# Grouping the score products of an attention pair, and dealing PSUM banks one by one

## The chip, the cores and the metric

The kernel runs on one core of a Trainium2 chip. A core has a matrix engine (TensorE, "PE" in the profile; its weight loads are "PEld"), a vector engine (VectorE, "DVE"), an engine for activations (ScalarE, "ACT"), a general one (GpSimd, "POOL"), a queue engine (SyncE, "SP") that here only issues DMAs, and 16 DMA engines. Matrix products are written to PSUM, an accumulator memory of 8 banks; a bank holds 512 float32 numbers on each of 128 partitions. The metric is the device time of one execution in microseconds (us), the median of several runs.

## What is computed

Eight sequences of 512 tokens of width 256 go through an attention layer with 16 heads of 64 and then through a gated feed-forward network with two hidden layers of 1024. All is float32. Only the attention part bears on the change:

```python
q = (x @ w_q).reshape(b, s, h, -1).transpose(0, 2, 1, 3)
kv = x @ w_kv
k, v = jnp.split(kv, 2, axis=-1)
...
q = _l2norm(q) * jnp.exp(scale)
k = _l2norm(k)
sim = jnp.einsum('bhid,bhjd->bhij', q, k)
attn = jax.nn.softmax(sim, axis=-1)
out = jnp.einsum('bhij,bhjd->bhid', attn, v)
out = out.transpose(0, 2, 1, 3).reshape(b, s, h * out.shape[-1])
return out @ w_out + b_out
...
x = x + _layernorm(_L0_attn_ref(_layernorm(x, axis=-1), ...), axis=-1)
x = x + _layernorm(_L0_ffn_ref(_layernorm(x, axis=-1), ...), axis=-1)
```

## The kernel before

**Stages.** The attention stage takes all eight sequences ("batches", `b`) one after the other, then the feed-forward network takes them in pairs. The attention stage writes its result to DRAM, and the feed-forward stage reads it back.

**Pairs.** Attention runs over 64 units of two heads, called pairs here, `(b, p)` with `p` from 0 to 7. Pairs 0 to 3 take the heads of the first half (`hf` 0), pairs 4 to 7 those of the second. For a pair:

- `scores(b, p, jb)` (lines 734 to 766), for each of four blocks `jb` of 128 keys: one product for each of the two heads (line 743), each with 64 rows of the array, so that both heads' products share it. The result `s` is a tile of two banks from the pool `ps_s`, which has two such tiles. Then ACT makes two exponentials (line 758), one for each head, into `e`; the key's inverse norm `kn` is the scale. There are five buffers of `e`, four of which a pair fills.
- `summed` (line 775), on DVE: the four blocks of `e` are added up in three additions into `es`.
- `values(b, p, jb)` (line 795): for each block and head a product with 64 columns of the array, accumulated over the four blocks in `po`, which has one bank (`ps_o`). `values_out` (line 891) copies it to `oT` on ACT. There are ten buffers of `oT`, eight of which a batch fills.
- `row_sums` (line 819), once for two pairs: the sums over keys, in products with 32 columns of the array, into `pd`; a copy `d`, a DMA that folds it, a reciprocal, a DMA to DRAM and two back spread it as `rden`, with which `normalised` (line 901) multiplies `oT`. Pairs 6 and 7 of the last batch use products with 64 columns and a reciprocal in place (`inverted`).

**Work beside the pairs.** Everything else of the stage is cut into steps, dealt to the pairs by the table `BESIDE` (lines 981 to 990), one string for each pair of a batch:

- `x`: a quarter of the next batch's input norm, with two transposes (`pt_a`, line 364).
- `t`: sums of tokens that the chains need.
- `c`: one product of a chain. A chain (`qk_chain`, from line 519; products at line 541) computes the queries or the keys of four pairs from seven products of quarter matrices in place of eight. Its products accumulate in PSUM banks called `g1`, `g2`, `g3`, and between them ACT copies a bank (`kept`, line 566), DVE adds a bank to a part made earlier (`added`, line 576), and ACT squares the result (`squared`, line 584). A product that goes on accumulating in a bank has to wait until the copy or addition of what is there has been done. There are four chains for each batch from the second on; the first is projected at the start.
- `q` and `k`: the sums of squares of queries or keys, in products with 32 columns (`norms_step`, line 633). For queries four DMAs, DVE work and a power on POOL (line 315) follow, and four DVE multiplications scale `qT`.
- `m`: the key norms: four transposes (`pk`, line 704), a DVE step and a power on POOL give `kn`.
- `v`: a quarter of the values of four pairs (`vp`, line 408), and a copy on ACT.
- `o`: a quarter of the output projection of the batch before (`pa`, line 922): eight products, then a norm on DVE and POOL.
- `l`: the issue of a load of a later batch.

Sums of the feed-forward weights (lines 1084 to 1140) also run there, on DVE and DMA; PE has no part in them.

**Order.** All steps are recorded by `steps.add(engine, length, run, reads, writes, takes, tiling)`. `Steps.issue` (line 84) then issues them. PE takes its steps strictly in the order in which they were recorded. Each other engine takes, of the steps that a model of the timing has ready, the one with the earliest latest start; what a step waits for follows from the parts of tiles that it reads and writes, and from the buffers that it takes.

For pair `u` and the pair ahead `n` the recorded order, which is PE's order, is: scores of `n`, blocks 0 and 1; values of `u` in four blocks; row sums at every second pair; scores of `n`, blocks 2 and 3; then the steps beside. The loop is at lines 1205 to 1234.

**PSUM.** Of the eight banks `ps_o` has one, `ps_s` four (two tiles of two), and `ps_w` three (`w0` to `w2`), which all other products share. `wbank` (line 325) deals these out, the least recently used first; a chain holds two of them (`hold=True`) from its first product to its last.

```python
    wbanks, held = [0, 1, 2], set()

    def wbank(hold=False):
        k = next(k for k in wbanks if k not in held)
        wbanks.remove(k)
        wbanks.append(k)
```

Below stand the functions that the diff touches, with the line numbers of the profile.

Of the kernel before, what the change touches and what calls it, by code (L numbers as in the profile page):

```python
# [17 lines left out]
P = 128  # L18
# [121 lines left out]
def tile_fast(  # L140
# [179 lines left out]

    wbanks, held = [0, 1, 2], set()

    def wbank(hold=False):
        k = next(k for k in wbanks if k not in held)
# [192 lines left out]
    def qk_chain(b, hf, which):  # L519
# [4 lines left out]
        g, tags = [("g1", *n), ("g2", *n), ("g3", *n)], {}  # L524

        def product(k, a, x, bank, fresh, last=False):
            if bank not in tags:
                tags[bank] = wbank(hold=True)
            tag = tags[bank]
            key = g[2] if k == 2 else g[bank]  # L530

            def run():
                if fresh:
                    tile_of(ps_w, [P, 2, HS], tag, key)
                w = quarter(which, hf, a)
                if x[0] == "T":
                    rhs = T[t][:, int(x[1]) - 1, :]
                else:
                    rhs = T["aT", b][:, int(x[1]) - 1, ts(int(x[2]) - 1, HS)]
                for o in range(2):  # L540
                    nc.tensor.matmul(  # L541
                        T[key][:, o, :], lhsT=w[:, ts(o, P)], rhs=rhs,
                        start=(fresh and o == 0), stop=True, skip_group_check=True,
                    )
# [12 lines left out]
            return key  # L557

        def part(i, k):
# [174 lines left out]
    def scores(b, p, jb):  # L734

        hf, j = divmod(p, HP)
        qT, kT, s, e = ("qT", b, hf), ("kT", b, hf), ("s", b, p, jb), ("e", b, p, jb)

        def products():
            tile_of(ps_s, [P, 2, S], "s", s)  # L740
            for h in range(2):
                hp = slice(h * DH, (h + 1) * DH)
                nc.tensor.matmul(  # L743
                    T[s][:, h, :],
                    lhsT=T[kT][hp, j, ts(jb, P)],
                    rhs=T[qT][hp, j, :],
                    start=True,
                    stop=True,
                )
# [5 lines left out]
        def exponentials():  # L755
            tile_of(ep, [P, 2, S], "e", e)
            for h in range(2):
                nc.scalar.activation(  # L758
                    T[e][:, h, :], T[s][:, h, :], AF.Exp,
                    scale=T["kn", b, hf][:, jb, 2 * j + h : 2 * j + h + 1],  # L760
                )

        steps.add(
            "act", 1.2, exponentials,
            reads=[(s, 0), (("kn", b, hf), 0)], writes=[(e, 0)], takes=[("e", NE, e)],
        )

    def summed(b, p, jb):

        t = ("es", b, p)  # L770

        def run():
            if jb == 1:
                tile_of(esp, [P, 2, S], "es", t)
            nc.vector.tensor_tensor(  # L775
                T[t], T["e", b, p, 0] if jb == 1 else T[t], T["e", b, p, jb], ALU.add
            )

        blocks = (0, 1) if jb == 1 else (jb,)
        steps.add(  # L780
            "dve", 1.22, run, reads=[(("e", b, p, i), 0) for i in blocks],
            writes=[(t, 0)], takes=[("es", 2, t)] if jb == 1 else (),
        )

    def values(b, p, jb):

        hf, j = divmod(p, HP)
        v, e, po = ("v", b, hf), ("e", b, p, jb), ("po", b, p)

        def products():  # L790
            if jb == 0:
                tile_of(ps_o, [P, S], "o", po)
            for h in range(2):
                c0 = j * P + h * DH
                nc.tensor.matmul(  # L795
                    T[po][h * DH : (h + 1) * DH, :],
                    lhsT=T[v][:, jb, c0 : c0 + DH],
                    rhs=T[e][:, h, :],
                    start=(jb == 0),
                    stop=(jb == NT - 1),  # L800
                )

        steps.add(
            "pe", 0.86, products, reads=[(e, 0), (v, jb)], writes=[(po, 0)],
            takes=[("o", 1, po)] if jb == 0 else (), tiling=("col", DH),
        )

# [97 lines left out]
    def out_proj(b, t, pairs=(0, NP), tail=False):  # L905

        pm, a, x = ("pa", b, t // 2 if tail else t), ("a", b, t), ("xres", b)
        st, mv, rs = ((n, b, t) for n in ("ost", "omv", "ors"))  # L910
        bank = None if tail else wbank()

        def banks():
            return T[pm][:, t % 2, :D] if tail else T[pm]

        def products():
            if pairs[0] == 0 and not tail:
                tile_of(ps_w, [P, D], bank, pm)
            elif pairs[0] == 0 and t % 2 == 0:
                tile_of(ps_s, [P, 2, S], "s", pm)  # L920
            for p in range(*pairs):
                nc.tensor.matmul(  # L922
                    banks(),
                    lhsT=T["oT", b, p][:, ts(t, P)],
                    rhs=wo_sb[:, p, :],
                    start=(p == 0),
                    stop=(p == NP - 1),
                )

        def biased():  # L930
            tile_of(rows, [P, D], "a", a)
            nc.vector.tensor_tensor(T[a], banks(), bo_sb, ALU.add)  # L932

        def stats():
            tile_of(small, [P, 6], "st1", st)
# [11 lines left out]

        takes = ()
        if pairs[0] == 0:
            takes = [(bank, 1, pm)] if not tail else [("s", 2, pm)] if t % 2 == 0 else ()  # L950
# [40 lines left out]
    plan = {}  # L991

# [206 lines left out]
        if t == 2:  # L1199
            key_norms(0, 1)  # L1200
    units = [(b, p) for b in range(B) for p in range(NP)]
    for g in range(2):
        for jb in (2 * g, 2 * g + 1):
            scores(*units[0], jb)
    for k, u in enumerate(units):
        ahead = units[k + 1 : k + 2]
        for jb in range(1, NT):
            summed(*u, jb)
        for g in range(2):
            for n in ahead:  # L1210
                for jb in (2 * g, 2 * g + 1):
                    scores(*n, jb)
            if g == 0:
                for jb in range(NT):
                    values(*u, jb)
                if not ahead:
                    for t in range(2):
                        out_proj(B - 1, t, (0, NP - 1), tail=True)
                b, p = u
                if (b, p // 2) == (B - 1, HP - 1):  # L1220
                    inverted(b, p)
                elif p % 2:
                    inverted_two(b, p - 1)
# [12 lines left out]
    for t in range(NT):  # L1236
# [3 lines left out]
    steps.add("pe", 0.0, lambda: None, reads=halves, tiling="full")  # L1240
    steps.add(
        "act", 1.5, lambda: nc.scalar.activation(top, top, AF.Silu),
        reads=[(("e", *units[-1], NT - 1), 0)],
    )
    for t in range(NT):
        out_proj(B - 1, t, (NP - 1, NP), tail=True)
    with tc.manual_schedule(engines=ORDERED):

        pm = ps_w.tile([P, S], F32, tag="w0", name="idle")
# [1000 lines left out]
```

## Time and profile before

| | us |
|---|---|
| median of 3 runs | 1607.86 (1606.53 to 1608.01) |
| the profiled execution | 1609.5 |
| its span, from the first to the last instruction | 1607.7 |
| PE busy in the span | 1587.7 |
| DVE, ACT, POOL busy | 1054.8, 927.8, 489.5 |
| values' last products in the attention stage | 985.9 |
| first product of the feed-forward stage | 1002.4 |

How to read it. The profile is of one execution. A row of a timeline has the start, the length, the engine, the line, what is written from what, the part of the array that is used (rows by columns), the shape and how many instructions were merged. A float32 product shows as two `MATMUL` instructions, since it is made in two passes. Starts are what was recorded; the ends of products are modelled, as products are pipelined, so a row may end after the next has begun. "Idle before" and the engine behind `<-` tell how long the engine had nothing to do and what ended it.

The PE clock that was granted is 0.996 of full speed in the mean of the span.

The groups that touch the change: 512 exponentials (line 758) have 316.7 us of ACT in all, 1024 score passes (line 743) 255.9 us of PE, 1024 value passes (line 795) 233.8 us, and the 192 sums of exponentials (line 775) 156.3 and 78.3 us of DVE.

### The profile page before, as it was taken

Reading aid. Unit: us, or ns where it says so; the run is one execution under the profiler, and the core shown is the slowest. Engines: PE = TensorE matmul, PEld = TensorE weight load, DVE = VectorE, ACT = ScalarE, POOL = GpSimd, SP = SyncE. Lnnn points to the kernel's source line nnn. Section 1 sums busy time; section 2 is a strip of 40 time slices with the busy share of each in tenths; the row PEclk is TensorE's granted clock in tenths of the full one; section 3 lists DMA queues with packets and bytes.
Section 4 is the critical chain, followed back from the end, with each engine's and each line's share of the span. In section 5 each row is a group of like instructions: output and inputs, shape, how many; then the busy total and the mean of one; then the engine's idle time right before and its main releaser. Section 6 shows DMA issues by size and latency. Waiting matters only on the chain.

```text
span 1607.7 us, 19708 instructions
## 1 busy us (share of the span) xinstructions
PE 1587.7 (99%) x7208; PEld 984.4 (61%) x7208; DVE 1054.8 (66%) x1772; ACT 927.8 (58%) x1543; POOL 489.5 (30%) x354
## 2 busy tenths in 40 slices
PE   9999999999999999999999999999999999999997
PEld 4344554454554554554554445788888888888886
DVE  4576776677454554554544365869787887879686
ACT  4666556556656556656646644566467646655663
POOL 4211312312302212212112120546165325625451
PEclk9999999999999999999999999999999999999998
DMA  5224323433211211121111310454324523441440
GB/s 175 54 80 124 110 97 94 119 106 80 54 40 41 48 46 41 42 53 41 41 53 41 93 54 19 143 155 147 120 77 131 170 92 103 145 139 60 140 149 29
DMA packets 77829, 142.66 MB, mean 89 GB/s; under 512 B 18844, under 2 KB 34460, under 8 KB 73628
## 3 DMA queue, kind: packets, MB, share of 16 engines
q1 hardware_dynamic: 58140, 78.40, 17.5%
q0 software_dynamic: 18880, 61.87, 12.4%
q8 instruction: 58, 0.95, 0.3%
q10 hardware_dynamic: 704, 1.05, 0.2%
q14 instruction: 47, 0.39, 0.1%
HBM read 123.49 MB, written 17.29 MB: 88 GB/s over the span
## 4 chain that ended last, share of the span: by engine, by line
PE 91%; DVE 4%; DMA 3%; ACT 1%; issue 1%; SPq 0%; DVEq 0%; ACTq 0%
PE g L1503 25%; PE s L743 14%; PE po L795 13%; PE p L1429 7%; PE vp L408 6%; PE pa L922 6%; PE g_k L541 5%; PE g_q L541 5%; PE py L1617 4%; PE pd L819 2%; DMA rden<-r 1%; DVE es L775 1%; PE pn_k L633 1%; PE pn_q L633 1%; PE kp L434 1%; PE qp L434 1%
## 5 line engine op out<-in xcount | busy, mean ns | idle before, releaser
L758 ACT ACTIVATE e<-s,kn 128x512 f32<-128x512 f32 x512 | 316.7, 686 | 183.4 <-PE s L743 144.6
L743 PE MATMUL s<-qT,kT 64*128 64x512 f32 x1024 | 255.9, 616 | 2.6 <-ACT e L758 2.4
L1503 PE MATMUL g<-h,wb_S 128*128 128x512 f32 x1024 | 234.2, 389 | 0.0
L795 PE MATMUL po<-e,v 128*64 128x512 f32 x1024 | 233.8, 598 | 0.0
L1503 PEld LDWEIGHTS g<-h,wb_S 128*128 128x128 f32 x1024 | 192.0, 188 | 39.8
L315 POOL TENSOR_TENSOR nf_q<-nf_q,neghalf 128x32 f32<-128x32 f32 x16 | 88.0, 5502 | 379.6 <-DVE nf_q L667 379.6
L775 DVE TENSOR_TENSOR es<-es,e 128x1024 f32<-128x1024 f32 x128 | 156.3, 1221 | 63.1 <-ACT e L758 57.6
L743 PEld LDWEIGHTS s<-qT,kT 64*128 64x128 f32 x1024 | 87.6, 186 | 145.4 <-issue 106.0
L1503 PE MATMUL g<-h,wb_A 128*128 128x512 f32 x768 | 176.4, 390 | 0.0
L775 DVE TENSOR_TENSOR es<-e,e 128x1024 f32<-128x1024 f32 x64 | 78.3, 1224 | 140.3 <-PE pd L819 102.4
L795 PEld LDWEIGHTS po<-e,v 128*64 128x64 f32 x1024 | 67.8, 136 | 158.2 <-issue 151.1
L1503 PEld LDWEIGHTS g<-h,wb_A 128*128 128x128 f32 x768 | 143.9, 188 | 29.9
L315 POOL TENSOR_TENSOR kn<-kn,neghalf 128x32 f32<-128x32 f32 x16 | 91.1, 5696 | 160.0 <-DVE kn L708 160.0
L1321 DVE TENSOR_TENSOR h<-C,h 128x512 fp32r<-128x512 f32 x112 | 129.5, 1211 | 3.9 <-ACT h L1311 3.8
L1321 DVE TENSOR_TENSOR h<-B,h 128x512 fp32r<-128x512 f32 x112 | 107.9, 1002 | 27.0 <-ACT h L1311 26.7
L408 PE MATMUL vp<-wv_sb,aT 128*128 128x512 f32 x256 | 120.8, 597 | 0.0
L922 PE MATMUL pa<-wo_sb,oT 128*128 128x256 f32 x512 | 116.0, 380 | 0.4 <-DVE a L932 0.4
L1559 POOL TENSOR_TENSOR B<-B,B 128x512 f32<-128x512 f32 x64 | 102.0, 1622 | 39.9 <-DVE B L1460 35.0
L922 PEld LDWEIGHTS pa<-wo_sb,oT 128*128 128x128 f32 x512 | 95.8, 190 | 16.2 <-issue 2.5
L1559 POOL TENSOR_TENSOR C<-C,C 128x512 f32<-128x512 f32 x64 | 94.1, 1496 | 27.7 <-DVE h L1321 27.2
L1528 ACT ACTIVATE C<-C,hs_sb 128x512 f32<-128x512 f32 x96 | 68.6, 722 | 47.7 <-DVE C L1550 47.5
L1550 DVE TENSOR_TENSOR C<-g,C 128x512 f32<-128x512 f32 x96 | 65.2, 687 | 45.1 <-PE g L1503 45.1
(170 smaller groups left out, 2234.9 us busy)
## 6 DMA issues: line engine op xcount, KB each, us to landing
wb_S<-s POOLq DMA_DIRECT2D x32, 1024.0 KB, 5.2
spread_q<-nq SPq DMA_DIRECT2D x32, 512.0 KB
rden<-r SPq DMA_DIRECT2D x62, 256.0 KB
wb_A<-in_h1T_dram POOLq DMA_DIRECT2D x12, 1024.0 KB, 5.5
wb_A<-in_h2T_dram POOLq DMA_DIRECT2D x12, 1024.0 KB, 5.5
s<-w SPq DMA_DIRECT2D x32, 256.0 KB
w<-in_h1T_dram SPq DMA_DIRECT2D x8, 512.0 KB
x<-xres SPq DMA_DIRECT2D x32, 128.0 KB
```

Source lines behind the costliest of these rows:

```text
L315: nc.gpsimd.tensor_tensor(d, d, neghalf.to_broadcast([P, n]), ALU.pow)
L408: nc.tensor.matmul(pm, lhsT=T["aT", b][:, c, ts(t, P)], rhs=w[:, c, c0 : c0 + HALF], start=(c == 0), stop=(c == ND - 1),)
L541: nc.tensor.matmul(T[key][:, o, :], lhsT=w[:, ts(o, P)], rhs=rhs, start=(fresh and o == 0), stop=True, skip_group_check=True,)
L743: nc.tensor.matmul(T[s][:, h, :], lhsT=T[kT][hp, j, ts(jb, P)], rhs=T[qT][hp, j, :], start=True, stop=True,)
L758: nc.scalar.activation(T[e][:, h, :], T[s][:, h, :], AF.Exp, scale=T["kn", b, hf][:, jb, 2 * j + h : 2 * j + h + 1],)
L775: nc.vector.tensor_tensor(T[t], T["e", b, p, 0] if jb == 1 else T[t], T["e", b, p, jb], ALU.add)
L795: nc.tensor.matmul(T[po][h * DH : (h + 1) * DH, :], lhsT=T[v][:, jb, c0 : c0 + DH], rhs=T[e][:, h, :], start=(jb == 0), stop=(jb == NT - 1),)
L922: nc.tensor.matmul(banks(), lhsT=T["oT", b, p][:, ts(t, P)], rhs=wo_sb[:, p, :], start=(p == 0), stop=(p == NP - 1),)
L1321: lambda: nc.vector.tensor_tensor(T[h][:, 1, c, :], T[raw][:, c, :], T[h][:, 0, c, :], ALU.subtract),
L1429: nc.tensor.matmul(T[ps[k]], lhsT=(w1r, w2r)[k][c][:, ts(o, P)], rhs=row_halves(b, i)[0][:, c, :], start=(c == 0 and i == 0), stop=(c == N ...
L1503: nc.tensor.matmul(T[to[o]], lhsT=T[w][:, c, ts(o, P)], rhs=T[h][:, i, c, :], start=(first and c == 0 and i == 0), stop=(c == NQ - 1 and i ...
L1559: lambda: (nc.gpsimd if T_ENGINE == "pool" else nc.vector).tensor_tensor(T[dst][:, c, :], T[x][:, c, :], T[y][:, c, :], ALU.subtract),
```

## The change

The scores of the pair ahead are all four recorded together, behind the values and row sums of the pair. Each head's scores have a tile of their own, of one bank, and the step of the two exponentials becomes two steps. The pool `ps_s` is gone, and its four banks go to `ps_w`, so that seven banks are dealt one by one, to scores and to all else. In a chain the bank `g3` is a bank of its own, `g2` is given back after the fourth step, and the sixth step runs ahead of the fifth. The table `BESIDE` is dealt anew: the seven products of a chain lie beside one pair (0, 2, 4 or 6), and the norms and key norms lie beside other pairs than before. At the end of the stage the output projection's last tiles use banks of `ps_w`.

```diff
-    ps_s = attn_scope.enter_context(tc.tile_pool(name="ps_s", bufs=2, space=PSUM))
...
-    wbanks, held = [0, 1, 2], set()
+    wbanks, held = list(range(7)), set()
...
         def product(k, a, x, bank, fresh, last=False):
-            if bank not in tags:
+            if fresh:
                 tags[bank] = wbank(hold=True)
-            tag = tags[bank]
-            key = g[2] if k == 2 else g[bank]
+            tag, key = tags[bank], g[bank]
...
-            if k == 2:
-                left_bank(tag)
-                held.add(int(tag[1]))
             if last:
                 left_bank(tag)
-                held.clear()
...
         def fourth():
-            added(0, 1, product(3, "S4", "B22", 1, False))
+            added(0, 1, product(3, "S4", "B22", 1, False, last=True))
...
         def sixth():
-            added(0, 0, product(2, "A12", "B21", 1, True))
+            added(0, 0, product(2, "A12", "B21", 2, True, last=True))
...
-        return [first, second, third, fourth, fifth, sixth, seventh]
+        return [first, second, third, fourth, sixth, fifth, seventh]
...
     def scores(b, p, jb):
-        qT, kT, s, e = ("qT", b, hf), ("kT", b, hf), ("s", b, p, jb), ("e", b, p, jb)
+        qT, kT, e = ("qT", b, hf), ("kT", b, hf), ("e", b, p, jb)
+        ss = [("s", b, p, jb, h) for h in range(2)]
+        tags = [wbank() for h in range(2)]

         def products():
-            tile_of(ps_s, [P, 2, S], "s", s)
             for h in range(2):
                 hp = slice(h * DH, (h + 1) * DH)
                 nc.tensor.matmul(
-                    T[s][:, h, :],
+                    tile_of(ps_w, [P, S], tags[h], ss[h]),
...
+        def exponential(h):
+            if h == 0:
+                tile_of(ep, [P, 2, S], "e", e)
+            nc.scalar.activation(
+                T[e][:, h, :], T[ss[h]], AF.Exp,
+                scale=T["kn", b, hf][:, jb, 2 * j + h : 2 * j + h + 1],
+            )
...
-            writes=[(s, 0)], takes=[("s", 2, s)], tiling="row",
...
+            writes=[(s, 0) for s in ss], takes=[(tags[h], 1, ss[h]) for h in range(2)], tiling="row",
+        )
+        for h in range(2):
+            steps.add(
+                "act", 0.6, lambda h=h: exponential(h),
+                reads=[(ss[h], 0), (("kn", b, hf), 0)], writes=[(e, h)],
+                takes=[("e", NE, e)] if h == 0 else (),
+            )
...
     BESIDE = (
-        "q c c x c x c x c v",
-        "k x o m o t",
-        "c c o c c o",
-        "c c v c v c c v l",
-        "q c c v c c c",
-        "k v m",
-        "c c v c c",
-        "c c v c c c",
+        "c c v c c c c v c x x x x",
+        "k o m o t",
+        "c c o c c c c o c",
+        "q v v l",
+        "c c v c c c c v c",
+        "k v",
+        "c c m c c c c v c",
+        "q",
     )
...
-        for g in range(2):
-            for n in ahead:
-                for jb in (2 * g, 2 * g + 1):
-                    scores(*n, jb)
-            if g == 0:
-                for jb in range(NT):
-                    values(*u, jb)
...
+        for jb in range(NT):
+            values(*u, jb)
...
+        for n in ahead:
+            for jb in range(NT):
+                scores(*n, jb)
         for g in range(2):
             for step in plan.pop(2 * k + g, []):
                 step()
```

More of the change, by code (lines that the diff above doesn't have):

```diff
@@ L749, in products @@
                 )
+        def exponential(h):
[5 more added lines that the diff above has]
+            )
         steps.add(
             "pe", 0.86, products, reads=[(kT, j), (qT, j)],
-            writes=[(s, 0)], takes=[("s", 2, s)], tiling="row",
+            writes=[(s, 0) for s in ss], takes=[(tags[h], 1, ss[h]) for h in range(2)], tiling="row",
         )
[L755 to L766, printed above, removed]
+        for h in range(2):
[4 more added lines that the diff above has]
+            )
     def summed(b, p, jb):
@@ L780, in summed @@
         steps.add(
-            "dve", 1.22, run, reads=[(("e", b, p, i), 0) for i in blocks],
+            "dve", 1.22, run, reads=[(("e", b, p, i), h) for i in blocks for h in range(2)],
             writes=[(t, 0)], takes=[("es", 2, t)] if jb == 1 else (),
@@ L803, in values @@
         steps.add(
-            "pe", 0.86, products, reads=[(e, 0), (v, jb)], writes=[(po, 0)],
+            "pe", 0.86, products, reads=[(e, 0), (e, 1), (v, jb)], writes=[(po, 0)],
             takes=[("o", 1, po)] if jb == 0 else (), tiling=("col", DH),
@@ L905, in out_proj @@
     def out_proj(b, t, pairs=(0, NP), tail=False):
-        pm, a, x = ("pa", b, t // 2 if tail else t), ("a", b, t), ("xres", b)
+        pm, a, x = ("pa", b, t), ("a", b, t), ("xres", b)
         st, mv, rs = ((n, b, t) for n in ("ost", "omv", "ors"))
-        bank = None if tail else wbank()
-        def banks():
-            return T[pm][:, t % 2, :D] if tail else T[pm]
+        bank = wbank(hold=tail) if pairs[0] == 0 else None
         def products():
-            if pairs[0] == 0 and not tail:
+            if pairs[0] == 0:
                 tile_of(ps_w, [P, D], bank, pm)
-            elif pairs[0] == 0 and t % 2 == 0:
-                tile_of(ps_s, [P, 2, S], "s", pm)
             for p in range(*pairs):
                 nc.tensor.matmul(
-                    banks(),
+                    T[pm],
                     lhsT=T["oT", b, p][:, ts(t, P)],
@@ L931, in biased @@
             tile_of(rows, [P, D], "a", a)
-            nc.vector.tensor_tensor(T[a], banks(), bo_sb, ALU.add)
+            nc.vector.tensor_tensor(T[a], T[pm], bo_sb, ALU.add)
         def stats():
@@ L949, in out_proj @@
         if pairs[0] == 0:
-            takes = [(bank, 1, pm)] if not tail else [("s", 2, pm)] if t % 2 == 0 else ()
+            takes = [(bank, 1, pm)]
         steps.add(
@@ L1201, in tile_fast @@
     units = [(b, p) for b in range(B) for p in range(NP)]
-    for g in range(2):
-        for jb in (2 * g, 2 * g + 1):
-            scores(*units[0], jb)
+    for jb in range(NT):
+        scores(*units[0], jb)
     for k, u in enumerate(units):
@@ L1208, in tile_fast @@
             summed(*u, jb)
-        for g in range(2):
-            for n in ahead:
-                for jb in (2 * g, 2 * g + 1):
-                    scores(*n, jb)
-            if g == 0:
-                for jb in range(NT):
-                    values(*u, jb)
[L1216 to L1223, printed above, removed]
+        for jb in range(NT):
+            values(*u, jb)
+        if not ahead:
+            for t in range(2):
+                out_proj(B - 1, t, (0, NP - 1), tail=True)
+        b, p = u
+        if (b, p // 2) == (B - 1, HP - 1):
+            inverted(b, p)
+        elif p % 2:
+            inverted_two(b, p - 1)
+        for n in ahead:
+            for jb in range(NT):
+                scores(*n, jb)
         for g in range(2):
@@ L1242, in tile_fast @@
         "act", 1.5, lambda: nc.scalar.activation(top, top, AF.Silu),
-        reads=[(("e", *units[-1], NT - 1), 0)],
+        reads=[(("e", *units[-1], NT - 1), 1)],
     )
@@ L1247, in tile_fast @@
     with tc.manual_schedule(engines=ORDERED):
-        pm = ps_w.tile([P, S], F32, tag="w0", name="idle")
+        pm = ps_w.tile([P, S], F32, tag="w6", name="idle")
         for _ in range(3):
```

## The prediction

> **What bounds the kernel now.** First the busy times and the chain that ended last. TensorE (PE) is busy nearly all the span and makes nine tenths of the chain; ACT and DVE have over a third of their time free.
>
> ```profile
> PE 1587.7 (99%) x7208; PEld 984.4 (61%) x7208; DVE 1054.8 (66%) x1772; ACT 927.8 (58%) x1543; POOL 489.5 (30%) x354
> ...
> PE 91%; DVE 4%; DMA 3%; ACT 1%; issue 1%; SPq 0%; DVEq 0%; ACTq 0%
> ```
>
> So what counts is PE time in the attention stage (0 to 1002 us; the gate and hidden layers behind it are not edited): the products, the changes of array shape between them, the waits. The edits remove no product: the two builds issue 2235 each up to the gate, in another order. The timeline of PE near the end of the stage prices the shapes:
>
> ```profile
> 950.95 5.42 PE L408 MATMUL vp<-wv_sb,aT 128*128 128x512 f32 x12
> 956.30 1.99 PE L743 MATMUL s<-qT,kT 64*128 64x512 f32 x8
> 958.22 3.65 PE L795 MATMUL po<-e,v 128*64 128x512 f32 x16
> 961.80 1.99 PE L743 MATMUL s<-qT,kT 64*128 64x512 f32 x8
> 964.36 2.29 PE L743 MATMUL s<-qT,kT 64*128 64x512 f32 x8 [0.57 <-ACT e L758]
> 966.57 3.65 PE L795 MATMUL po<-e,v 128*64 128x512 f32 x16
> 970.15 1.06 PE L819 MATMUL pd<-es,ones 128*32 128x512 f32 x8
> 971.15 1.99 PE L743 MATMUL s<-qT,kT 64*128 64x512 f32 x8
> ```
>
> Read the starts, since a row's length runs past the next start. A float32 product is two passes of 0.429 us per 512 columns (single starts in the trace); the two heads' score or value products run side by side (7 ns apart), the four of a row sum too. The visit to the full array from 950.95 takes 5.35 us for 12 passes (5.15): 0.20 for the visit. Scores, 956.30 to 958.22: 1.92 against 4 passes (1.72), 0.20. Values, 3.58 against 8 passes (3.43), 0.15. Row sums, 1.00 against 2 (0.86), 0.14. Single starts split each into leaving and entering: full 93 and 104 ns (56 for transposes), row halves (scores) 97 and 104, column halves (values) 100 and 51, column quarters 113 and 24. With these every start in the stage comes out within 12 ns, except at real waits. The views of waits and groups:
>
> ```profile
> PE s L743 <- ACT e L758: 2.4, 5, 0.9
> ...
> PE g_k L541 <- DVE kT L576: 1.0, 1, 1.0
> ...
> PE g_k L541 <- DVE qT L576: 0.6, 1, 0.6
> ...
> PE g_q L541 <- DVE qT L576: 0.5, 1, 0.5
> ```
>
> ```profile
> L758 ACT ACTIVATE e<-s,kn 128x512 f32<-128x512 f32 x512 | 316.7, 686 | 183.4 <-PE s L743 144.6
> ...
> L775 DVE TENSOR_TENSOR es<-es,e 128x1024 f32<-128x1024 f32 x128 | 156.3, 1221 | 63.1 <-ACT e L758 57.6
> ```
>
> These waits are understated: a product may start 0.16 us before the row ahead of it ends, and after a wait the weight load is no longer ahead (0.10 us more). At 964.36 the plan by passes was 963.63, so 0.73 is lost and 0.29 more in the group: 1.0 for the 0.57 shown. By starts the stage loses 5.6 us before scores and 5.9 in the chains (L541) and the output product behind them.
>
> **The change, part by part.**
>
> *Shape changes.* Before, a pair runs scores, values, (row sums), scores, beside; after, values, (row sums), scores, beside. Counted in the two builds' order: visits for scores fall from 124 to 64, -60 x 0.201 = -12.1. Visits to the full array fall from 67 to 58, seven of the nine for transposes: -7 x 0.149 - 2 x 0.197 = -1.4. Values 65 and row sums with norms 63 stay. Together -13.5. One junction is nearly new: full array to values, 52 against 1. Leaving and entering give 0.144, as in its one row. Bounds from the nearest rows: full to column quarters 0.117, column halves to full 0.204, so -1.4 to +3.1 over 51; I take 0.144, since every other junction adds up.
>
> *Seven banks dealt singly, one tile per head.* The score waits came of two score tiles: a third block waited for the exponentials of the first. Now the eighth bank of a pair comes back with its first exponential: from the start of scores, 1.24 to the first exponential (trace, 319.59 to 320.83) plus 0.58, so 1.8, needed at 2.6. The 5.6 us go. What is late next: in a pair with nothing beside, values. ACT makes a block's two exponentials in 1.154 (0.585 and 0.569 back to back), so the blocks are ready at 2.4, 3.5, 4.7, 5.85. Values follow at 3.63, 4.54, 5.40, 6.26: 0.4 us to spare with ACT free at 1.24 (a value copy or row-sum copy of 0.59 ends at 0.75). No wait.
>
> The score product of each head now has its own wait and increment, and each exponential its own wait. I cost this at nothing, by the norm products of the start-up, where three of four weight loads wait and three products increment, against a set with one of each:
>
> ```profile
> 25.04 1.07 PE L633 MATMUL pn_k<-spread_k,halves_of 128*32 128x512 f32 x8
> ...
> 305.38 1.06 PE L633 MATMUL pn_k<-spread_k,halves_of 128*32 128x512 f32 x8
> ```
>
> By these rows 0.01 us for two increments more, at most 1.3 over 256 blocks. The Trainium skill ("TensorE: Matmul & The Clock Gate", section "The cost: per-tile semaphore tail") speaks against the change: increments serialize, and it puts 26.3 ns on each; an estimate by it is 256 x 0.0263 = 6.7 us more, a total of 1597. The rows above do not show it on PE's path.
>
> *Sums behind values.* Where nothing lies beside (pairs 5 and 6 of the last batch), row sums follow values and need the third DVE sum: 1.22 each, the first at 3.65, so the last ends at 7.3; row sums were due at 7.2. About 0.2 with the weight load, twice: +0.4. Elsewhere the pair ahead had a long list beside.
>
> *Chains inside one pair.* First and second products, then v, output product or key-norm transposes, then third, fourth, sixth, fifth, another filler, seventh. The third writes the bank that ACT copies from, and that copy now stands behind seven exponentials: 1.24 + 3 x 1.154 + 0.585 = 5.28, plus 0.60 and 0.05 to PE, 5.94. With v (1.72) between, the third is due at 7.2: hidden. With transposes (0.44) it is due at 5.90: 0.14 with the weight load, in 7 pairs: +1.0. Queued behind it on PE: the chain and the next values. The seventh needs a DVE add (0.69) after the fifth, now with v (1.72) or an output product (3.45) between, before at times one chain product (0.86); but DVE sums of 1.22 and additions that wait for DMA stand in its queue. I keep the 5.9 us of chain waits; bounds none and twice that.
>
> *Values in pair 2* need their one bank, whose copy needs an oT buffer read last by the output product just before the seventh. Copy done 1.12 us after that product's last start (0.38 + 0.10 + 0.59 + 0.05), values due at 1.17. No wait.
>
> *Moved steps.* Query norms run one pair earlier (their four DMAs on SP each with them, past row-sum DMAs), with four pairs of 10 to 17 us until use. Half the key norms move a pair later, POOL's 5.5 us (kn rows of the page, 5696 ns) with them: from their transposes at 5.9, done at about 13; the next batch's scores start at 16.7, exponentials at 17.9. Without that cover the price is what is late, up to 5.7 us x 7. Nothing is added on SP or POOL.
>
> **Sum:** -13.5 - 5.6 + 0.4 + 1.0 = -17.7. The profiled execution took 1609.5 (its span 1607.7, 1.8 around it): 1591.8. It lies 1.6 above the median of the runs shown, 1607.86, so against that median 1590.2, rounded 1590.5.
>
> **The rivals.**
>
> 1. *New waits eat a part.* Heads of the DVE and ACT queues that wait for DMA meet the chains as they do at 157 and 907 us now. Chain waits doubled (+5.9), the new junction at its dear end (+3.1): 1593 to 1600, say 1596. For: DVE is over 70% busy from 100 to 400 us. Against: most fillers grew. 0.25.
> 2. *The chain waits go too*, as their fillers are longer: 1590.5 - 5.9 = 1584.6. For: in the steady batches the only one left is 0.19 at a seventh product one product behind the fifth. Against: the large ones (0.77 at 101 us, 1.29 at 907) come of late DVE queues. 0.12.
> 3. *Increments cost PE time*: +1.3 by the rows: 1592. 0.03. The skill's rule above is this one, with its own price.
> 4. *Slower: the burst of exponentials makes ACT late at the third product.* Place: the 28 chain pairs, where the copy stands behind seven exponentials. With v between, ACT has 1.2 us to spare. Slower than before begins where these 28 lose 17.4/28 = 0.6 each, so with ACT some 1.8 late; at 2.5 late, 28 x 1.4 = 39: 1590 + 39 = 1629. Against: ahead of those scores come values without row sums, and ACT has only an oT copy of 0.59 to do. 0.04.
> 5. *The heads no longer run side by side* once each has its own tile. Then each block takes two passes more, 256 x 0.86 = 220: 1810. Against: the norm rows at 25.04. 0.02.
>
> **How the numbers follow.** Forecast 1590.5 with 0.54, its own range 1587 to 1594; the rivals as above. 1585 to 1600 holds the forecast, rival 3, most of rival 1 and about half of rival 2, some 0.83. From no change the measurement can tell about 0.2%, 3.2 us. Faster by more: all but rivals 4, 5 and a sliver of 1, 0.92; within, 0.02; slower 0.06.
>
> **What would show it.** Score rows of 16 in one visit, 3.63 us from start to the next shape; no PE wait of scores for e; values after chains entered at about 0.14; PE's attention stage some 17 us shorter and the stages behind it of the same length. Score rows of twice the length show rival 5; chain products waiting for ACT copies show rival 4; waits for DVE in the chains over 6 us show rival 1. The prediction is wrong if scores still wait, if waits of values for e appear in most pairs, or if the gate stage gives the gain back.

## The result, and the profile after

The changed kernel takes 1587.93 us (median of 4 runs, 1587.26 to 1589.02) against 1607.93 (4 runs beside it, 1606.53 to 1608.54): a ratio of 0.9877, with a 95% interval of 0.986 to 0.9895. That is 20.0 us less. Its profiled execution took 1589.0, with a span of 1587.2, 20.5 less than the span before; the granted PE clock is 0.998.

The busy times and the engines' shares of the chain that ended last:

```profile
PE 1569.8 (99%) x7208; PEld 992.9 (63%) x7208; DVE 1059.5 (67%) x1772; ACT 915.8 (58%) x1543; POOL 493.4 (31%) x354
...
PE 96%; DVE 3%; ACT 0%; issue 0%; DMA 0%; DVEq 0%
```

PE has the same 7208 instructions, is busy 17.9 us less, and now makes 96% of the chain (91% before): the kernel is bound by PE even more than it was. The timeline of PE near the end of the attention stage, as it was shown of before (start, length, line, what from what, part of the array, shape, count):

```profile
934.75 3.70 PE L407 MATMUL vp<-wv_sb,aT 128*128 128x512 f32 x8
938.39 3.65 PE L792 MATMUL po<-e,v 128*64 128x512 f32 x16
941.97 3.70 PE L738 MATMUL s<-qT,kT 64*128 64x512 f32 x16
945.60 3.65 PE L792 MATMUL po<-e,v 128*64 128x512 f32 x16
949.19 1.39 PE L816 MATMUL pd<-es,ones 128*32 128x512 f32 x8
950.51 3.70 PE L738 MATMUL s<-qT,kT 64*128 64x512 f32 x16
954.14 3.65 PE L792 MATMUL po<-e,v 128*64 128x512 f32 x16
958.06 1.08 PE L816 MATMUL pd<-es,ones 128*64 128x512 f32 x4 [0.27 <-DVE es L772]
959.07 3.70 PE L738 MATMUL s<-qT,kT 64*128 64x512 f32 x16
```

Read the starts again. A pair's scores are one visit: 941.97 to 945.60 is 3.63 us for 16 instructions, which is 8 passes of 0.429 (3.43) and one change of shape, 0.20, where before there were two. No score row carries a wait. The row sums at 949.19 and 958.06 are the place where no work lies beside. The first row starts in time, but its later products come 0.3 late (it is 1.39 long in place of 1.07); the second row loses 0.49. Both wait for a DVE sum that has not ended. The waits of PE (us in total, times, longest):

```profile
PE g_k L539 <- DVE kT L570: 1.5, 2, 0.8
PE p L1418 <- issue: 1.4, 1, 1.4
PE g_q L539 <- DVE qT L570: 0.8, 1, 0.8
...
PE pd L816 <- DVE es L772: 0.3, 1, 0.3
...
PE g_q L539 <- ACT qT L560: 0.2, 1, 0.2
```

The scores' waits for `e` (2.4 us in the view before) are gone. What is left in the chains is three waits for DVE additions that are long enough for this view and one for an ACT copy. New is one wait of 1.4 us at the first product of the feed-forward stage (L1418). The exponentials and the sums over them, to be put beside the two groups in the prediction's working, and the first sum of each pair, before (L775) and after (L772):

```profile
L749 ACT ACTIVATE e<-s,kn 128x512 f32<-128x512 f32 x512 | 308.5, 703 | 100.1 <-PE s L738 100.1
...
L772 DVE TENSOR_TENSOR es<-es,e 128x1024 f32<-128x1024 f32 x128 | 156.7, 1224 | 18.6 <-ACT e L749 8.5
...
L772 DVE TENSOR_TENSOR es<-e,e 128x1024 f32<-128x1024 f32 x64 | 78.1, 1221 | 63.4 <-ACT e L749 63.2
```

```profile
L775 DVE TENSOR_TENSOR es<-e,e 128x1024 f32<-128x1024 f32 x64 | 78.3, 1224 | 140.3 <-PE pd L819 102.4
```

ACT makes the same 512 exponentials, eight in a row, and stands idle before them for 100.1 us, not 183.4. DVE's waits have moved: ahead of the second and third sum of a pair it now stands 18.6 us (63.1 before), and ahead of the first one 63.4, nearly all for ACT, where before it stood 140.3, mostly put down to PE's row sums. Together that is 82 us for 203, on an engine that is not the bound.

Where the 20.5 us of the span came from, by PE's starts:

| | before | after | |
|---|---|---|---|
| start to the last output product (`pa`) | 1002.35 | 982.78 | -19.6 |
| of it, changes of array shape | 56.2 | 42.7 | -13.5 |
| of it, waits of scores | 5.3 | 0.1 | -5.2 |
| of it, waits in chains and of the output product behind them | 5.9 | 4.0 | -1.9 |
| of it, row sums waiting for DVE sums | 0 | 0.8 | +0.8 |
| last output product to the end | 605.36 | 604.45 | -0.9 |

The four parts add up to -19.8, 0.2 more than the -19.6 measured. The price of a change of shape is taken from the trace before; with it nearly every start in the new order comes out within some 12 ns, except at the waits and in the first 9 us. The new junction, full array to column halves, is entered 52 times at 0.144 each. The last row of the table compares unlike clocks: in the profiled execution before, PE ran at half clock for 3.4 us early in the gate stage, in the one after it did not (last section). That drop costs some 1.6 us; by that estimate the part behind the last output product is about 0.7 longer after the change at the same clock, not 0.9 shorter. So the gain is the attention stage's, and the 20.0 of the medians is a fairer figure than the 20.5 of the two profiled spans.

### The profile page after: what moved, and what is told of

Same layout as the page of the kernel before. It is cut to its first block, busy times and chain, and to the rows that moved or that the text cites. A ratio compares the mean times of both kernels' runs of the same rounds, so it can differ in the third digit from the quotient of the medians.

```text
span 1587.2 us, 19688 instructions
## 1 busy us (share of the span) xinstructions
PE 1569.8 (99%) x7208; PEld 992.9 (63%) x7208; DVE 1059.5 (67%) x1772; ACT 915.8 (58%) x1543; POOL 493.4 (31%) x354
## 3 DMA queue, kind: packets, MB, share of 16 engines
q1 hardware_dynamic: 58140, 78.40, 17.7%
q10 hardware_dynamic: 704, 1.05, 0.2%
## 4 chain that ended last, share of the span: by engine, by line
PE 96%; DVE 3%; ACT 0%; issue 0%; DMA 0%; DVEq 0%
PE g L1492 26%; PE s L738 14%; PE po L792 14%; PE pa L914 7%; PE vp L407 7%; PE p L1418 6%; PE g_q L539 5%; PE g_k L539 5%; PE py L1606 4%; PE pd L816 2%; PE pn_q L627 1%; PE pn_k L627 1%; PE kp L433 1%; PE qp L433 1%; PE pt_a L363 0%; PE pk L698 0%
## 5 line engine op out<-in xcount | busy, mean ns | idle before, releaser
L749 ACT ACTIVATE e<-s,kn 128x512 f32<-128x512 f32 x512 | 308.5, 703 | 100.1 <-PE s L738 100.1
L738 PE MATMUL s<-qT,kT 64*128 64x512 f32 x1024 | 237.1, 602 | 0.0
L738 PEld LDWEIGHTS s<-qT,kT 64*128 64x128 f32 x1024 | 93.6, 186 | 143.2 <-issue 135.3
L772 DVE TENSOR_TENSOR es<-es,e 128x1024 f32<-128x1024 f32 x128 | 156.7, 1224 | 18.6 <-ACT e L749 8.5
L314 POOL TENSOR_TENSOR kn<-kn,neghalf 128x32 f32<-128x32 f32 x16 | 87.5, 5470 | 241.5 <-DVE kn L702 241.5
L772 DVE TENSOR_TENSOR es<-e,e 128x1024 f32<-128x1024 f32 x64 | 78.1, 1221 | 63.4 <-ACT e L749 63.2
L888 ACT COPY oT<-po 128x512 f32<-128x512 f32 x64 | 37.4, 585 | 125.8 <-PE po L792 123.9
L914 PEld LDWEIGHTS pa<-wo_sb,oT 128*128 128x128 f32 x512 | 95.8, 190 | 20.5 <-ACT e L749 6.6
```

The lines of the kernel that those rows point to most:

```text
L314: nc.gpsimd.tensor_tensor(d, d, neghalf.to_broadcast([P, n]), ALU.pow)
L738: nc.tensor.matmul(tile_of(ps_w, [P, S], tags[h], ss[h]), lhsT=T[kT][hp, j, ts(jb, P)], rhs=T[qT][hp, j, :], start=True, stop=True,)
L749: nc.scalar.activation(T[e][:, h, :], T[ss[h]], AF.Exp, scale=T["kn", b, hf][:, jb, 2 * j + h : 2 * j + h + 1],)
L772: nc.vector.tensor_tensor(T[t], T["e", b, p, 0] if jb == 1 else T[t], T["e", b, p, jb], ALU.add)
L914: nc.tensor.matmul(T[pm], lhsT=T["oT", b, p][:, ts(t, P)], rhs=wo_sb[:, p, :], start=(p == 0), stop=(p == NP - 1),)
```

## Experiments

**1. Scores in two visits again.** The changed kernel, but the first two score blocks ahead of the values and the last two behind, as before the change. Banks, tiles, chains and table stay.

```diff
+        for n in ahead:
+            for jb in (0, 1):
+                scores(*n, jb)
         for jb in range(NT):
             values(*u, jb)
...
-            for jb in range(NT):
+            for jb in (2, 3):
                 scores(*n, jb)
```

> The changed kernel with one part undone: scores of the pair ahead stand again as two blocks before the values and two behind them; banks, chains and table stay. Theory (the gain is shape changes, 0.201 us for each visit of the scores): 59 visits more, +11.9 us, so 1587.9 + 11.9 = 1599.8 (1598 to 1601.5), and no PE wait of scores for e. Rival (the gain is mostly the seven banks and the new table): below 1594. Rival (the burst of exponentials costs something that the split takes away): also below 1598.

1598.45 us (ratio to before 0.994, 0.9923 to 0.9956), 10.5 above the changed kernel. The order has 123 score visits for 64, 11.9 us by the shape prices; in exchange the chains' waits fell from 4.0 to 2.4: the two at 237 and 291 us are gone, probably since more work lies ahead of the late additions there. The span is 9.9 longer; 11.9 - 1.6 = 10.3. The grouping's price holds, and over half of the gain hangs on it.

**2. The grouping alone.** The kernel before with only its recorded order changed: values, row sums, all four score blocks. Two score tiles of two banks, the old chains and table.

```diff
-        for g in range(2):
-            for n in ahead:
-                for jb in (2 * g, 2 * g + 1):
-                    scores(*n, jb)
...
+        for jb in range(NT):
+            values(*u, jb)
...
+        for n in ahead:
+            for jb in range(NT):
+                scores(*n, jb)
```

> The kernel before with one part done: only the order of the scores is changed (all four blocks behind the values); two score tiles of two banks, three other banks, old table and chains. Theory (grouping needs the single banks, as a third block waits for the exponentials of the first): visits -12.1, but each of 63 pairs loses about 1.0 at its third and fourth block, as 961.80 to 966.57 us of the kernel before did (4.77 for two groups of two against 3.73): +65 - 5 for the waits that were there; 1607.9 + 48 = 1656 (1640 to 1670). Rival (the waits hide, the grouping pays by itself): 1594 to 1600.

1668.21 us (1.0372, 1.0354 to 1.0389): 61 us slower than the kernel before. Its PE waits, and a place in its PE timeline:

```profile
PE s L743 <- ACT e L758: 34.1, 64, 0.9
PE pa L922 <- DVE a L932: 3.4, 2, 3.1
PE g_q L541 <- DVE qT L576: 3.1, 3, 2.6
```

```profile
402.33 3.65 PE L795 MATMUL po<-e,v 128*64 128x512 f32 x16
405.91 1.99 PE L743 MATMUL s<-qT,kT 64*128 64x512 f32 x8
408.41 2.28 PE L743 MATMUL s<-qT,kT 64*128 64x512 f32 x8 [0.51 <-ACT e L758]
410.62 1.13 PE L541 MATMUL g_q<-aT,wq_sb 128*128 128x256 f32 x4
```

The third block waits in each of 64 pairs: its place in PSUM is that of the first block, whose exponentials are not done. The view shows 0.51; by the starts, the group from 405.91 to 410.62 takes 4.71 in place of 3.63, so a wait of about 1.1 in each pair. In all, scores wait 70.5 us (5.3 before), the chains and output products 5 more than before, and the shapes give 12.1 back: 65.2 + 5 - 12.1 = 58, near the 61 measured. The expected 1656 had too low a price for the waits; the direction and the range (1640 to 1670) stand.

**3. The banks alone.** The kernel before with the seven banks dealt one by one, a tile and a step for each head, and the last output projection's tiles in the shared pool; the old order, chains and table.

```diff
-    ps_s = attn_scope.enter_context(tc.tile_pool(name="ps_s", bufs=2, space=PSUM))
...
-    wbanks, held = [0, 1, 2], set()
+    wbanks, held = list(range(7)), set()
...
-            tile_of(ps_s, [P, 2, S], "s", s)
...
-                    T[s][:, h, :],
+                    tile_of(ps_w, [P, S], tags[h], ss[h]),
```

> The kernel before with the other part done: seven banks dealt singly and a tile and an exponential step for each head; order of the scores, chains and table as before. Theory (banks alone only take the 5.6 us of score waits): 1602.4; the end of the stage as in the changed kernel (1.8 more at the hand-over, 3.0 less in the first gate steps) 1601.2; so 1600 to 1603.5. Rival (the banks bring most of the 20 us): below 1596. Rival (separate increments and waits cost PE time, 256 x 26 ns): 1608 or more.

1602.54 us (0.9967, 0.9954 to 0.9979). The scores' waits are gone and the shapes are as before. The rival with a price on each increment (1608 or more) is out. So the banks by themselves are worth 5 us; the grouping without them costs 61, and with them it gives 10.5. The 4.1 us that are left, from this run to experiment 1, belong to the new table and chains together (by starts, shape changes 1.6 less and chain waits some 2.3 less); the two were not tried apart, but for the order of two products in experiment 4.

**4. The fifth chain product ahead of the sixth again.**

```diff
-        return [first, second, third, fourth, sixth, fifth, seventh]
+        return [first, second, third, fourth, fifth, sixth, seventh]
```

> The changed kernel with the chain's fifth step ahead of its sixth again. The fifth product then goes on in the bank of the third with one chain product (0.86 us) between them, and the ACT copy of the third needs 0.38 + 0.10 + 0.60 + 0.05 = 1.13 from the third's last start, where 1.08 is left: a wait of 0.05 to 0.2 in each of 28 chains. Theory: +1.4 to +5.6, 1589.3 to 1593.5, by PE waits of the chain for ACT. Rival (the order of these two does nothing): 1587.9 within 0.7.

1588.14 us (0.9876, 0.986 to 0.9893), level with the changed kernel: the theory is out by its total. Its PE timeline at one of the chains with a late addition, and the changed kernel's at the same chain:

```profile
285.94 1.11 PE L539 MATMUL g_k<-tsum,wk_sb 128*128 128x256 f32 x4
286.88 1.03 PE L539 MATMUL g_k<-aT,wk_sb 128*128 128x256 f32 x4
287.75 1.88 PE L407 MATMUL vp<-wv_sb,aT 128*128 128x512 f32 x4
289.46 1.03 PE L539 MATMUL g_k<-tsum,wk_sb 128*128 128x256 f32 x4
```

```profile
286.88 1.03 PE L539 MATMUL g_k<-aT,wk_sb 128*128 128x256 f32 x4
287.75 1.03 PE L539 MATMUL g_k<-tsum,wk_sb 128*128 128x256 f32 x4
288.61 1.88 PE L407 MATMUL vp<-wv_sb,aT 128*128 128x512 f32 x4
291.33 1.13 PE L539 MATMUL g_k<-tsum,wk_sb 128*128 128x256 f32 x4 [0.84 <-DVE kT L570]
```

The small wait that the new order avoids is real: the fifth product's group is 0.94 from start to start (285.94 to 286.88) in place of 0.86, as it writes the bank that ACT is still copying; that is 0.08 in 27 chains, 2.1 us. But with the fifth product first its addition comes first in DVE's queue too, and the seventh follows its filler at 289.46 without a wait, where the changed kernel loses 1.1 us at 291.33. The two orders pay the same in different coin.

**5. Where the late additions come from.** DVE in the changed kernel, ahead of that wait:

```profile
276.10 1.23 DVE L772 TENSOR_TENSOR es<-es,e 128x1024 f32<-128x1024 f32 x1
280.81 0.18 DVE L661 TENSOR_SCALAR nf_q<-nf_q 128x32 f32<-128x32 f32 x1 [3.49 <-DMA nf_q<-nd_q]
...
286.91 0.24 DVE L667 TENSOR_SCALAR nf_q<-nf_q,escale 128x32 f32<-128x32 f32 x1 [1.61 <-POOL nf_q L314]
...
289.40 1.88 DVE L570 TENSOR_TENSOR kT<-g_k,kT 128x512 f32<-128x512 f32 x3
```

DVE stands 3.49 us for the DMA that folds the query norms (issued at 276.2, landed by 280.8: 4.6 us, where the planner counts 1.8), and 1.61 more for POOL's power. Behind these in its queue lie the additions of 289.40, for which PE waits. If the places of these steps in the queue are the cause, a planner that knows the DMA's length puts other work first:

```diff
-            "sync", 0.1, folded, reads=[(d, 0)], writes=[(f, 0)], takes=[("nf", 2, f)], lag=1.8
+            "sync", 0.1, folded, reads=[(d, 0)], writes=[(f, 0)], takes=[("nf", 2, f)], lag=4.5
```

> The changed kernel with one number of the plan changed: the DMA that folds the query norms is taken to land 4.5 us after its issue, not 1.8 (it took 4.6 at 276.2 us of the changed kernel, with DVE standing 3.5 us behind it). No instruction is added, only DVE's and ACT's order moves. Theory (the chain waits of 0.95 at 237 us and 1.1 at 291 us are DVE's queue standing behind these norms): these go, 1587.9 - 2.1 = 1585.8 (1585 to 1586.8). Rival (they come of the load of DVE as such): 1587.5 or more, with waits elsewhere.

1586.88 us (0.9869, 0.9854 to 0.9885), 0.1 above the theory's range and 1.05 below the changed kernel. The trace decides: both waits are gone (237 and 291 us), the chains' waits fall from 4.0 to 1.9, and the span is 1585.0, 2.2 less. That the order of DVE's queue makes these two waits is shown; its worth in the median is one microsecond, less than the 1.8 between the changed kernel's fastest and slowest run. The same place in this version, where the seventh product follows the filler at once, on PE and then on DVE:

```profile
287.64 1.88 PE L407 MATMUL vp<-wv_sb,aT 128*128 128x512 f32 x4
289.36 1.03 PE L539 MATMUL g_k<-tsum,wk_sb 128*128 128x256 f32 x4
```

```profile
279.32 1.29 DVE L898 TENSOR_TENSOR oT<-oT,rden 128x512 f32<-128x512 f32 x2 [2.97 <-DMA rden<-r]
...
286.18 1.49 DVE L570 TENSOR_TENSOR kT<-g_k,kT 128x512 f32<-128x512 f32 x2
287.58 0.23 DVE L667 TENSOR_SCALAR nf_q<-nf_q,escale 128x32 f32<-128x32 f32 x1
```

The fold DMA itself is not what goes away: DVE still stands 2.97 us, now for the DMA of `rden`, which is half a microsecond less. What goes is mainly the 1.61 for POOL, since two of the three additions now come ahead of the norm step that needs POOL's power. At 237 us it is the other way round: there DVE stood 0.84 us for the fold and not at all for POOL, and the 0.84 is gone.

**6. One more kind of visit removed.** If the price of a shape is what counts, then norm products recorded right behind row sums, which use the same column quarters, should save 28 of 63 visits, 3.8 us.

```diff
+        if kind in "qk":
+            early.setdefault(u, []).append(step)
+        else:
+            at(2 * u, step)
...
+        for step in early.pop(k, []):
+            step()
```

> The changed kernel with the query and key norm products moved from behind the scores to right behind the row sums, which use the same 32-column shape. Theory (PE pays by visits): 28 visits fewer at 0.113 + 0.024 = 0.137, -3.8 us, so 1584.1 (1583 to 1585.3), if the squares that the norms read are ready (1.9 us earlier need, about 2.5 us to spare by rows). Rival (the price of a visit was an effect of something else, or the norms now wait for ACT): 1587 to 1590.

1584.68 us (0.9854, 0.9839 to 0.9869), 3.25 below the changed kernel, with a span 4.0 shorter. With experiment 5's lag on top:

> Both of the last two: norms behind the row sums, and the fold taken to land at 4.5 us. If both theories hold and don't meet, -3.8 - 2.1: 1582.0 (1581 to 1583.5). If the earlier norms bring their DVE work elsewhere and the lag does nothing, 1584.

1582.72 us (5 runs, 1582.57 to 1583.3; 0.9844, 0.9831 to 0.9857): the fastest version found, 5.2 below the changed kernel.

**7. The gap ahead of the feed-forward stage.** The changed kernel's PE timeline at the border:

```profile
981.27 1.89 PE L914 MATMUL pa<-wo_sb,oT 128*128 128x256 f32 x8
984.58 0.47 PE L1418 MATMUL p<-fT,w1r 128*128 128x512 f32 x1 [1.43 <-issue]
```

From the last start of `pa` (982.78) to the first product of the gate 1.80 us pass; before it was 0.03. All versions with the seven banks in one pool have this gap. From the first gate product to the end they take 602.0 to 602.7 us, the profiled execution before 605.3, but 1.6 of that are its half clock. A first try put the tiles of the last output products in four fixed banks:

```diff
-        bank = wbank(hold=tail) if pairs[0] == 0 else None
+        bank = None
+        if pairs[0] == 0 and tail:
+            if t == 0:
+                held.update((2, 3, 4, 5))
+            bank = f"w{2 + t}"
+        elif pairs[0] == 0:
+            bank = wbank()
```

> The changed kernel with the last output projections in four banks that the first gate products don't use, as in the kernel before. Theory (the 1.8 us wait at the hand-over lets DVE and ACT get ahead, and is more than given back: from the last output product to the end 604.0 to 604.5 us with the wait, 605.4 to 605.6 without it): no wait at the hand-over, but the waits for B and sg and some 3.4 us of half clock in the first gate steps are back; 1587.9 + 1.2 = 1589.1 (1588.5 to 1590). Rival (the wait is a plain loss): 1586.1 to 1586.5.

1588.2 us (0.9875, 0.986 to 0.9891), and the gap stayed at 1.8, so this run tells nothing of what the gap costs. The second try split the seven banks into two pools and put those tiles in the second:

```diff
+    ps_v = attn_scope.enter_context(tc.tile_pool(name="ps_v", bufs=1, space=PSUM))
...
+    def ps_of(tag):
+        return ps_v if int(tag[1]) < 3 else ps_w
...
-                tile_of(ps_w, [P, D], bank, pm)
+                tile_of(ps_of(bank), [P, D], bank, pm)
...
+                held.update((3, 4, 5, 6))
+            bank = f"w{3 + t}"
```

> The changed kernel with its seven shared banks in two pools, of three and of four banks, still dealt one by one; the last four output-projection tiles lie in the pool of four, so that the first gate bank belongs only to banks that are free. Theory (the 1.8 us gap before the first gate product is a wait for the pool of the last tiles, and costs nothing in the end, since the gate stage gets it back): the gap falls from 1.8 us to under 0.1; the first 20 us of the gate then show again the waits for DVE (1.0 us) and 3.4 us of half clock that the kernel before has; from the last output product to the end 605.4 in place of 604.4, total 1587.9 to 1589.5. Rival (the gap is a plain loss): no new waits behind it, 602.7 from the last output product to the end, total 1585.8 to 1586.6. If the gap stays, it is not a wait for these banks.

1587.68 us (0.9872, 0.9857 to 0.9887), level with the changed kernel: not the rival's 1585.8 to 1586.6, and 0.2 under the theory's range, as the stage ahead came 0.9 shorter with banks dealt this way. The gap is gone, and the waits of before are back:

```profile
980.35 1.89 PE L925 MATMUL pa<-wo_sb,oT 128*128 128x256 f32 x8
981.89 0.58 PE L1429 MATMUL p<-fT,w1r 128*128 128x512 f32 x1
...
993.00 0.50 PE L1429 MATMUL p<-fT,w1r 128*128 128x512 f32 x1 [0.99 <-DVE B L1460]
...
994.76 0.69 PE L1429 MATMUL p<-fT,w2r 128*128 128x512 f32 x1 [0.57 <-ACT sg L1450]
995.25 0.63 PE L1429 MATMUL p<-fL,w2r 128*128 128x512 f32 x1
995.67 0.63 PE L1429 MATMUL p<-fT,w2r 128*128 128x512 f32 x1
```

The gate's start is late for its data in either case: a wait of 1.8 us at the border takes the place of waits of 1.0 and 0.6 some ten us later. From the last output product to the end it is 604.9 here and 605.4 before, both with 1.6 of half clock behind those waits, and 604.45 with the gap. The same split on the fastest version:

> The same two pools on top of the version with norms behind row sums and the longer lag of the fold. Theory (the gap is given back): 1582.5 to 1584.5. Rival (plain loss): 1580.5 to 1581.5.

1582.9 us (5 runs, 1582.54 to 1583.4; 0.9843, 0.9829 to 0.9856), as without it. The profiled execution has no gap, kept full clock at the border, and takes 603.4 from the last output product to the end, where the eight versions with the gap take 603.8 to 604.5. So at the same clock the gap may cost 0.4 to 1 us; the medians show no loss.

## Why the prediction was right

The forecast of 1590.5 (the sum gave 1590.2, rounded up) lay 2.6 above the measured time, near the low end of its own range of 1587 to 1594. The mechanism was right in its two large terms; the chains were mis-sized. Point by point:

- *Shape changes, -13.5.* Measured -13.5 by the starts, and experiments 1 and 6 price visits by themselves: 59 more score visits cost 9.9 of span with 1.6 of waits saved, 28 fewer visits of column quarters saved 4.0 of span for 3.8 reckoned.
- *The new junction, 0.144.* Every one of the 52 took that. The bounds (0.117 and 0.204) were not needed.
- *Score waits, -5.6.* Measured -5.2. Experiment 3 gets them without the grouping, and experiment 2 shows what the grouping does without the banks: the two parts of the change are no sum, as the second pays for the first.
- *Split waits and increments at nothing.* Held: 16 instructions in 3.63 us, as with one tile for both heads, and the two heads still start 7 ns apart (rivals 3 and 5 are out). The Trainium skill's 26.3 ns for each increment ("TensorE: Matmul & The Clock Gate", section "The cost: per-tile semaphore tail") would have made each such visit 0.1 us longer by estimate; no run here shows it on PE's path.
- *Sums behind values, +0.4.* Measured 0.8, in the two places named. Right place, size off by a factor of two.
- *Third product of the chain, +1.0.* It waits in seven pairs as foreseen, but for 0.05, not 0.14: 0.3 in all. The 0.10 for a weight load that is no longer ahead was charged to a wait too short to cost it.
- *Chain waits kept at 5.9.* This is the largest term off: they are some 3.7 without the third product, and 4.0 with it. Rival 2 (all go) and rival 1 (they double) were both wrong in size; what is left are mainly four waits of 0.5 to 1.1, of which the two at 237 and 291 us come of the order of DVE's queue around the query norms, as experiment 5 shows. The other two, at 85 and 90 us, were not tried.
- *Values in pair 2, moved steps.* No wait for them is to be seen. ACT is late at the third product by the 0.05 above, and once, at 85 us, by 0.4 in a chain that has no filler ahead of that product; rival 4, which had this in 28 chains, is out.
- *What the prediction left out:* the border to the feed-forward stage. That "the gate and hidden layers behind it are not edited" holds for their code, but their first product now waits 1.8 us for what the last output products hold (one bank or the whole pool: the fixed banks of the first try did not help, the second pool did). It did little harm because the data behind it was late anyhow, by experiment 7; that this would be so was luck, not forecast.

By these terms: 17.7 were foreseen, and the four measured parts make 19.8. The chains are 2.9 better than the sum had them (+1.0 foreseen, -1.9 measured); score waits and row sums, 0.4 worse each, take 0.8 of that back. So the errors cancel in part. The 0.9 that brings the span to 20.5 is the clock of the one execution before.

## What to carry to other kernels

Where PE is the bound and shapes alternate, count visits, price each by start-to-start times of single junctions, and multiply: here that term came out to the tenth of a microsecond, while the waits did not. A grouping that saves visits needs room for its results: the same reordering lost 61 us with PSUM dealt in pairs of banks and won 10.5 with banks dealt singly, so the two must be judged together. A wait newly shown ahead of a stage is a loss only if that stage was not about to wait for something else; remove it and look at what comes next before counting it.

## What the hardware did that was not expected

At the start of the gate stage the PE clock drops in some executions. Granted clock by stretch (us, busy us, clock, DMA share, GB/s), of the kernel before, and of the version with two pools:

```profile
1002.38:1022.00 19.62, 18.03 (x74) 0.91 0.89 279
```

```profile
981.89:1001.00 19.11, 17.55 (x72) 0.91 0.97 296
```

For 3.4 us products there start 0.43 us apart in place of 0.23. It begins with the product after the two waits of 1.0 and 0.6 us. The changed kernel, with the gap and without these waits, has a clock of 1.00 there:

```profile
984.58:1002.00 17.42, 16.80 (x75) 1.00 1.10 335
```

But the fastest version with two pools has both waits and full clock:

```profile
977.29:996.00 18.71, 16.92 (x76) 1.00 0.92 290
```

So the waits alone do not bring the drop; what does is open. It is a matter of the execution, not of the kernel alone. In the traces the mean clock is 0.996 where the drop is there, and 0.997 or 0.998 where it is not. Of 40 executions of versions without the gap (27 of them of the kernel before) seven have 0.996, four of the kernel before among them, at 1608.8 to 1611.3 us; its 23 others have a median of 1607.4. Of 35 executions with the gap none has 0.996. The drop makes 1.6 us of difference in the first 64 products of the stage: 19.4 us with the waits and the drop, 17.8 with the waits alone, 16.0 behind the gap.
